# A selective scan on VectorE: two states in one scan over two PSUM banks, instead of one state over one bank

## The chip, the cores and the metric

One NeuronCore of a Trainium2 chip runs the whole program in one launch. The time is device microseconds of an execution, the median of three runs. The profile shows one further execution. Engines are named as the profile names them: PE is TensorE, DVE is VectorE, ACT is ScalarE, POOL is GpSimd, SP is SyncE, which issues the DMAs.

## The reference

Eight images of 96 channels and 64 x 64 pixels pass through a layer with a selective scan and then through attention and a feed-forward part. The scan takes nearly all the time. For each image there are four directions k (row order, column order, and both reversed), 192 channels d, 16 states n and 4096 positions:

```python
def step(hst, inp):
    u_i, dt_i, b_i, c_i = inp
    dA = jnp.exp(dt_i[..., None] * A)
    hst = dA * hst + (dt_i * u_i)[..., None] * b_i[:, :, None, :]
    y = jnp.einsum('bkdn,bkn->bkd', hst, c_i)
    return (hst, y)
h0 = jnp.zeros((bb, k, d, n), u.dtype)
_, ys = lax.scan(step, h0, (u_t, dt_t, b_t, c_t))
return ys.transpose(1, 2, 3, 0) + D[None, :, :, None] * u
```

Before it, per image, come a normalization, a projection, a depthwise convolution and the projections that give the step sizes dt, B and C ("front"). After it come a gate, two convolutions with a channel gate, attention, and a quantized feed-forward ("back end").

## The kernel before, in words

**Units, tiles, states, slots.** A *unit* is one direction of one image on one chunk of T = 512 positions: 8 images x 4 directions x 8 chunks = 256 units. A unit has six *tiles* n = 0 to 5 (`TILES`: g is a half of the states, j a third of the channels). The 128 partitions of a tile hold 64 channels twice, each half with other states, and its free axis holds G = 4 states m of 512 positions. So a unit has 24 *slots*, slot = 4n + m, and each slot is one scan of 128 x 512.

**The way of one state.**
- `inputs` (L952): POOL multiplies B by dt * u for all four states of a tile into an SBUF buffer `hb` (six buffers). It is issued two tiles ahead.
- `decays` (L1065): ACT writes exp(dt * A) of one state into one PSUM bank `da`, issued two slots ahead. There are three such banks.
- the scan (L1133): DVE runs h = da * h + hb along the 512 positions. A column of `carry` holds h from the chunk before. The first chunk of a direction starts from 0.
- the product with C: for some states DVE does it, right after the scan (L1135). Those are the *banked* states: their scan writes its result back into the PSUM bank `da`, and the product reads that bank and writes `hb`. For the other states the scan writes `hb`, and POOL later multiplies a tile's unbanked states in one instruction (`outputs`, L962).
- the carry: ACT copies the last column of each banked scan (L1136), or of a tile's unbanked scans together (L1141). These copies wait in `kept` and are issued at the beginning of the next slot.
- `sums` (L972): PE adds the states up with a matmul against `halves`, in PSUM banks y01 and y2. A last matmul adds D * u, or the sum of the directions before (`ident`), and `gather` (L993) has ACT copy the bank out for a DMA.

`BANKED` (L34) says how many states of each tile are banked: tiles 0, 2 and 4 all four, 1 and 3 none, tile 5 two, or one in the first eight units of images 1 to 7.

**Step sizes** (`step_sizes`, L911) have six steps i: a matmul into PSUM, then Abs, Exp and Ln on ACT (softplus), a combination on DVE, and dt * u on POOL. They come once a unit for 128 channels (kind "a") and once in two units for the other 64 of both (kind "b", in odd units). `spread` (L940) has SP copy the results within SBUF into the layout of the tiles. `states` loads B and C, `fetched_dt`, `fetched_u` and `fetched_pair` load what the step sizes need, `before` (L964) loads the operand of the last matmul.

**The order is written by hand.** `plan` (L1007) puts each of these calls for the unit `u`, its predecessor `last` and its successors `nxt` and `third` at a slot. The loop from L1102 issues, in each slot: the carry copies kept, the exp of two slots later, the scan, the product with C, and what the plan has there. Every engine takes its instructions in this order. After that `advance` lets two side streams go on: the front of the next image and the back end of the image before. They put a few matmuls, activations and DVE products into the slots. A side stream that needs another activation table waits for one of the slots `CALM = (0, 1, 8, 9, 16, 17)`, and then loads a table, runs Silu or Gelu, and loads the old table again. Before the units of the next image are fetched, the front of that image is drained.

[...] three for `da`, one for `dt` (step sizes), one each for f0 and f1 (side streams), y01 and y2.

Of the kernel before, what the change touches and what calls it, by code (L numbers as in the profile page):

```python
# [24 lines left out]
G = 4  # L25
# [8 lines left out]
BANKED = ((4, 0, 4, 0, 4, 1), (4, 0, 4, 0, 4, 2))  # L34
# [9 lines left out]
def kernel(ctx: ExitStack, tc: tile.TileContext, a, out):  # L44
# [16 lines left out]
    BANKS = {"da": 3, "dt": 1, "f0": 1, "f1": 1, "y01": 1, "y2": 1}  # L61
# [14 lines left out]
    one = const([P, 1], 1.0, "one")  # L76
    ones_c = const([C, C], 1.0 / C, "ones_c")
# [778 lines left out]
    for b in range(out.shape[0]):  # L856
        s = {"b": b, "done": set(), "live": b + 1 == out.shape[0]}
        images.append(s)
        for pair in (1, 0):
            for back in range(2):  # L860
                for i in range(NC):
                    u = Unit()
                    u.s, u.pair, u.back, u.k = s, pair, back, pair + 2 * back
                    u.c, u.start = (NC - 1 - i if back else i), i == 0
                    u.new, u.i = (pair, back, i) == (1, 0, 0), len(units)
                    u.bc, u.hb, u.delta, u.du = {}, {}, {}, {}
                    u.banked = BANKED[int(b == 0 or u.i % 32 >= NC)]
                    units.append(u)
# [42 lines left out]
    def step_sizes(us, i):  # L911

        u, which = us[0], "ab"[len(us) - 1]
        if i == 0:
            u.ps = bank("dt", "dt")
            if which == "a":
                todo = [(u.ps, slice(0, P), u)]
            else:
                todo = [(u.ps[64 * h : 64 * h + 64], slice(P, DI), w) for h, w in enumerate(us)]
            for ps, d, w in todo:  # L920
                nc.tensor.matmul(ps, dt_w[32 * w.k : 32 * w.k + R + 1, d], w.dts, start=True, stop=True)  # L921
            u.nat = sp.tile([P, T], F32, tag="nat" + which, name="nat", bufs=1)
            if which == "a":
                u.nata = u.nat
            else:
                for w in us:
                    w.natb = u.nat
        elif i == 1:
            nc.scalar.activation(u.nat, u.ps, AF.Abs)
        elif i == 2:  # L930
            nc.scalar.activation(u.nat, u.nat, AF.Exp, scale=-1.0)
        elif i == 3:
            nc.scalar.activation(u.nat, u.nat, AF.Ln, bias=one)  # L933
        elif i == 4:
            nc.vector.scalar_tensor_tensor(u.nat, u.ps, 0.0, u.nat, ALU.max, ALU.add)  # L935
        else:
            x = u.ua if which == "a" else u.ub
            nc.gpsimd.tensor_tensor(x, u.nat, x, ALU.mult)  # L938
# [19 lines left out]
    def outputs(u, n):  # L958

        lo = u.banked[n]  # L960
        hb = u.hb[n][:, lo:, :]
        nc.gpsimd.tensor_tensor(hb, hb, u.bc[1, TILES[n][0]][:, lo:, :], ALU.mult)  # L962

    def before(u):  # L964

        src = u.s["u"][1] if u.k == 1 else u.s["y"][u.pair]
        u.plain = []
        for i, rows in enumerate((slice(0, P), slice(P, src.shape[0]))):
            t = sp.tile([P, T], F32, tag=f"u{i}", name=f"u{i}", bufs=1)[: rows.stop - rows.start]
            u.plain.append(into(t, src[rows, bass.ts(u.c, T)]))  # L970

    def sums(u, ns, m):  # L972
# [12 lines left out]
        if ns[-1] == 5 and m == 1:  # L985
            first = u.k == 1
            for ps, w, x in (
                (u.p[0], dd_a if first else ident, u.plain[0]),
                (u.p[1][low] if first else u.p[1], dd_b if first else ident, u.plain[1]),
            ):  # L990
                nc.tensor.matmul(ps, w, x, start=False, stop=True, skip_group_check=True)  # L991
# [15 lines left out]
    def plan(u, last, nxt, third):  # L1007
# [6 lines left out]
        if last:  # L1014
            put(0, outputs, last, 5)
            put(0, before, last)
            for m in range(2):
                put(m, sums, last, (3, 4), 2 + m)
            for m in range(2):
                put(5 + m, sums, last, (5,), m)  # L1020
            put(7, states, u, 1, 1)
            put(10, gather, last, 0)
            put(11, gather, last, 1)
# [4 lines left out]
        if third and u.i % 2:  # L1028
            put(16, step_sizes, (nxt, third), 5)
        put(8, outputs, u, 1)  # L1030
        put(16, outputs, u, 3)
        for m in range(4):
            put(13 + m, sums, u, (0, 1), m)
            if m < 2:
                put(18 + m, sums, u, (2,), m)
                put(22 + m, sums, u, (3, 4), m)
        if nxt:
            for i, slot in enumerate((0, 2, 4)):
                put(slot, step_sizes, (nxt,), i + 3)
            put(4, spread, nxt, 0, (0, 1))  # L1040
            put(6, spread, nxt, 1, (0, 1))
# [6 lines left out]
        if third:  # L1048
            put(1, fetched_dt, third)
            put(9, fetched_u, third)  # L1050
            for i, slot in enumerate((20, 22, 23)):
                put(slot, step_sizes, (third,), i)
            if u.i % 2:
                for i, slot in enumerate((9, 11, 12, 13, 15)):
                    put(slot, step_sizes, (nxt, third), i)
                put(17, spread, nxt, 0, (2,))
                put(18, spread, nxt, 1, (2,))
            elif u.i + 3 < len(units):
                put(21, fetched_pair, third, units[u.i + 3])
        return at  # L1060

    def at_index(i):
        return units[i] if 0 <= i < len(units) else None

    def decays(q):  # L1065

        if q >= 24 * len(units):
# [3 lines left out]
        da[q] = bank("da", "da")  # L1071
        nc.scalar.activation(  # L1072
            da[q], u.delta[j], AF.Exp, scale=a_neg[:, u.k, j, g * G + m : g * G + m + 1]
        )

    da, kept, side, carry = {}, [], [], None
# [12 lines left out]
    for i in range(3):  # L1089
        step_sizes(units[1:2], i)  # L1090
# [3 lines left out]
    decays(1)  # L1094

# [6 lines left out]
    for u in units:  # L1102
# [13 lines left out]
        if third and third.new:  # L1116
            drained(*side[-1:])
            all_issued()
        if u.start:
            carry = sp.tile([P, 24], F32, tag="carry", name="carry")  # L1120
        todo = plan(u, last, nxt, third)
        for slot in range(24):
            n, m = divmod(slot, G)
            g, j = TILES[n]
            q, hb, first_at = 24 * u.i + slot, u.hb[n], 0 if u.back else T - 1
            col = carry[:, 8 * j + g * G + m : 8 * j + g * G + m + 1]
            while kept:
                kept.pop(0)()
            decays(q + 2)
            d = da.pop(q)  # L1130
            banked = m < u.banked[n]
            dd, x = (d[:, ::-1], hb[:, m, ::-1]) if u.back else (d, hb[:, m, :])
            nc.vector.tensor_tensor_scan(dd if banked else x, dd, x, 0.0 if u.start else col, ALU.mult, ALU.add)  # L1133
            if banked:
                nc.vector.tensor_tensor(hb[:, m, :], d, u.bc[1, g][:, m, :], ALU.mult)  # L1135
                kept.append(lambda col=col, d=d, at=first_at: nc.scalar.copy(col, d[:, at : at + 1]))  # L1136
            elif m == G - 1:
                lo = 8 * j + g * G
                kept.append(
                    lambda c=carry[:, lo + u.banked[n] : lo + G].unsqueeze(2), h=hb[:, u.banked[n] :, :], at=first_at:  # L1140
                    nc.scalar.copy(c, h[:, :, at : at + 1])  # L1141
                )
# [8 lines left out]
    before(u)  # L1151
    for m in range(2):
        sums(u, (3, 4), 2 + m)
    for m in range(2):
        sums(u, (5,), m)
    gather(u, 0)
# [79 lines left out]
```

## Time and profile before

| | us |
|---|---|
| median of three runs | 11327.45 (11326.49 to 11333.61) |
| profiled execution, its own time | 11335.55 |
| its span, first to last instruction | 11333.8 |
| first scan to last scan | about 352 to 11,091 |

| engine | busy us in the profile | what takes it |
|---|---|---|
| DVE | 10390.3 | 6144 scans, 3528 products with C |
| POOL | 10398.8 | 1536 input products, 768 output products |
| PE | 8544.5 | sums, side streams |
| ACT | 7478.7 | 6144 exps, carry copies, side streams |

A line of the groups reads: source line, engine, operation, tile written <- tiles read, shapes, count, then busy us and mean ns of one, then the engine's idle time just before such instructions and what ended most of it. A line of the waits reads: who waited <- for whom: us in total, times, longest. A line of the timeline: start, duration, engine, instruction. A line of the windows: stretch, its length, then the busy us of each engine with the number of its instructions, the granted TensorE clock, the share of the DMA engines and GB/s.

### The profile page before, as it was taken

How to read it: one execution, taken by the hardware profiler on the slowest of the kernel's cores; microseconds unless marked ns; L12 is line 12 of the kernel's file. 1: busy time of each engine (PE TensorE's matmuls, PEld its weight loads, DVE VectorE, ACT ScalarE, POOL GpSimd, SP SyncE). 2: the span in 40 equal slices, each digit the busy share in tenths (PEclk: the TensorE clock that was granted, in tenths of full speed). 3: DMA queues.
4: the chain of work that ended last, by engine and by line, in shares of the span. 5: the costliest groups of instructions: out<-in, count | busy, mean ns of one | idle time of the engine just before them, and what ended most of it. 6: DMA issues, size and time to landing. Idle time of an engine off the chain costs nothing. (4 is left out here: it accounts for less than half of the span.)

```text
span 11333.8 us, 97039 instructions
## 1 busy us (share of the span) xinstructions
PE 8544.5 (75%) x23270; PEld 2320.9 (20%) x23270; DVE 10390.3 (92%) x10868; ACT 7478.7 (66%) x14899; POOL 10398.8 (92%) x2783
## 2 busy tenths in 40 slices
PE   6577658887678876888678876788768877676677
PEld 2111112222122211222112221222212221111212
DVE  0799999999999999999999999999999999999993
ACT  3566656767666676667766676666766667666674
POOL 0799999999999999999999999999999999999991
PEclk8678878888788877889788887888878888787788
DMA  2788878898888888888888888889888888888883
GB/s 70 170 197 197 200 188 210 208 226 200 202 207 211 221 198 201 212 212 216 195 212 207 214 217 195 208 205 224 213 197 207 211 220 201 195 199 196 202 199 90
DMA packets 1081040, 2253.25 MB, mean 199 GB/s; under 512 B 419609, under 2 KB 420314, under 8 KB 949395
## 3 DMA queue, kind: packets, MB, share of 16 engines
q1 hardware_dynamic: 1080467, 2247.05, 81.5%
q8 instruction: 184, 3.01, 0.1%
q14 instruction: 389, 3.19, 0.1%
HBM read 1507.14 MB, written 336.69 MB: 163 GB/s over the span
## 5 line engine op out<-in xcount | busy, mean ns | idle before, releaser
L956 POOL TENSOR_TENSOR hb<-b,du 128x2048 f32<-128x2048 f32 x1536 | 6935.8, 4532 | 23.0 <-DMA du<-ua 16.0
L1072 ACT ACTIVATE da<-delta,w_a_logs 128x512 f32<-128x512 f32 x6144 | 4216.4, 689 | 696.7 <-DVE hb L1133 575.6
L982 PE MATMUL p<-hb,halves 128*64 128x512 f32 x12288 | 3813.9, 729 | 809.0 <-POOL hb L962 391.7
L1133 DVE TENSOR_TENSOR_SCAN da<-da,carry,hb 128x512 f32<-128x512 f32 x3087 | 3949.2, 1279 | 57.1 <-ACT da L1072 53.4
L962 POOL TENSOR_TENSOR hb<-hb,c 128x2048 f32<-128x2048 f32 (+2 forms) x768 | 2982.3, 3883 | 304.7 <-ACT carry L1141 262.6
L1133 DVE TENSOR_TENSOR_SCAN hb<-da,carry,hb 128x512 f32<-128x512 f32 x2289 | 2781.1, 1264 | 59.4 <-ACT da L1072 58.4
L1135 DVE TENSOR_TENSOR hb<-da,c 128x512 f32<-128x512 f32 x3528 | 2440.6, 692 | 153.9 <-DVE da L1133 0.9
L1136 ACT COPY carry<-da 128x1 f32<-128x1 f32 x3528 | 554.8, 157 | 2356.0 <-DVE hb L1135 2345.5
L982 PEld LDWEIGHTS p<-hb,halves 128*64 128x64 f32 x12288 | 914.5, 161 | 3556.5 <-issue 2126.2
L435 PE MATMUL conv<-f0im,taps 97*128 97x512 f32 (+1 forms) x2088 | 909.3, 669 | 89.8 <-ACT f0pre L491 50.3
L1133 DVE TENSOR_TENSOR_SCAN da<-da,hb 128x512 f32<-128x512 f32 x441 | 537.8, 1219 | 27.9 <-POOL hb L956 26.5
L938 POOL TENSOR_TENSOR ua<-nat,ua 128x512 f32<-128x512 f32 x256 | 326.7, 1276 | 257.6 <-DMA b<-xd 257.6
L935 DVE SCALAR_TENSOR_TENSOR nat<-dt,nat 128x512 f32<-128x512 f32 x384 | 259.5, 676 | 239.3 <-ACT nat L933 239.3
L921 PE MATMUL dt<-dts,dt_w 7*64 7x512 f32 (+1 forms) x1024 | 450.8, 660 | 18.8 <-DVE nat L935 14.3
L991 PE MATMUL p<-u,ident 128*128 128x512 f32 x768 | 436.0, 695 | 5.3 <-DMA u<-y 5.1
L376 PE MATMUL ctr<-f1b,cen_c 96*96 96x512 f32 x460 | 271.0, 695 | 198.8 <-DVE f1b L770 160.6
L435 PEld LDWEIGHTS conv<-f0im,taps 97*128 97x128 f32 (+1 forms) x2088 | 254.5, 175 | 676.4 <-issue 524.4
L1133 DVE TENSOR_TENSOR_SCAN hb<-da,hb 128x512 f32<-128x512 f32 x327 | 377.9, 1204 | 4.9 <-ACT da L1072 4.9
L382 PE MATMUL var<-f1b,ones_c 96*96 96x512 f32 x346 | 207.9, 685 | 152.6 <-ACT f1b L379 143.0
L1141 ACT COPY carry<-hb 128x4 f32<-128x4 f32 (+2 forms) x768 | 146.7, 191 | 197.3 <-DVE hb L1133 184.8
L656 PE MATMUL cab<-f1m,cab_w 96*96 96x512 f32 x348 | 206.0, 719 | 91.1 <-ACT f1b L665 41.7
L619 PE MATMUL cab<-f1im,cab_w 97*32 97x512 f32 x1044 | 264.7, 627 | 12.8 <-DMA f1im<-xld 7.9
(425 smaller groups left out, 7479.0 us busy)
## 6 DMA issues: line engine op xcount, KB each, us to landing
b<-xd SPq DMA_DIRECT2D x1024, 512.0 KB
c<-xd SPq DMA_DIRECT2D x1024, 512.0 KB
delta<-nat SPq DMA_DIRECT2D x1536, 128.0 KB
du<-ua SPq DMA_DIRECT2D x1024, 128.0 KB
y<-yt SPq DMA_DIRECT2D x512, 256.0 KB
u<-y SPq DMA_DIRECT2D x384, 256.0 KB
ua<-u SPq DMA_DIRECT2D x256, 256.0 KB
du<-ub SPq DMA_DIRECT2D x512, 128.0 KB
```

The lines of the kernel that those rows point to most:

```text
L376: nc.tensor.matmul(ps, cen_c, src, start=i == 0, stop=i == len(srcs) - 1)
L435: nc.tensor.matmul(ps, taps[:, t, lo : lo + n], im[:, r0 + dy : r0 + dy + 8, dx : dx + HW], start=t == 0, stop=t == 8,)
L921: nc.tensor.matmul(ps, dt_w[32 * w.k : 32 * w.k + R + 1, d], w.dts, start=True, stop=True)
L938: nc.gpsimd.tensor_tensor(x, u.nat, x, ALU.mult)
L956: nc.gpsimd.tensor_tensor(hb, u.bc[0, g], u.du[j].unsqueeze(1).to_broadcast([P, G, T]), ALU.mult)
L962: nc.gpsimd.tensor_tensor(hb, hb, u.bc[1, TILES[n][0]][:, lo:, :], ALU.mult)
L982: nc.tensor.matmul(ps, halves, u.hb[n][:, i, :], start=TILES[n][0] == 0 and m == 0, stop=False, skip_group_check=True)
L991: nc.tensor.matmul(ps, w, x, start=False, stop=True, skip_group_check=True)
L1072: nc.scalar.activation(da[q], u.delta[j], AF.Exp, scale=a_neg[:, u.k, j, g * G + m : g * G + m + 1])
L1133: nc.vector.tensor_tensor_scan(dd if banked else x, dd, x, 0.0 if u.start else col, ALU.mult, ALU.add)
L1135: nc.vector.tensor_tensor(hb[:, m, :], d, u.bc[1, g][:, m, :], ALU.mult)
L1136: kept.append(lambda col=col, d=d, at=first_at: nc.scalar.copy(col, d[:, at : at + 1]))
```

## The change

Banked states are taken in pairs. A tile `da` now holds two states over two PSUM banks, and two such tiles replace the three single banks. One scan of 1024 elements runs through both states, one product with C covers both, and one copy saves both carries; it is issued at the beginning of the slot after the pair's second one. So that the second state of a pair starts afresh, ACT adds its decay times its carry to its first input element and then sets that decay to 0. Unbanked states keep a scan each. Odd units (but for the first eight of images 1 to 7) have all four states of tile 5 banked, and no POOL product for it. The bank `dt` goes: step sizes use y01 and y2 between the gather of one unit and the sums of the next, and the plan is rearranged for that.

```diff
-BANKED = ((4, 0, 4, 0, 4, 1), (4, 0, 4, 0, 4, 2))
+BANKED = (((4, 0, 4, 0, 4, 2),), ((4, 0, 4, 0, 4, 2), (4, 0, 4, 0, 4, 4)))
...
-    BANKS = {"da": 3, "dt": 1, "f0": 1, "f1": 1, "y01": 1, "y2": 1}
+    BANKS = {"f0": 1, "f1": 1, "y01": 1, "y2": 1}
...
-                    u.banked = BANKED[int(b == 0 or u.i % 32 >= NC)]
+                    some = BANKED[int(b == 0 or u.i % 32 >= NC)]
+                    u.banked = some[u.i % len(some)]
...
-            u.ps = bank("dt", "dt")
+            u.ps = bank({"a": "y01", "b": "y2"}[which], "dt")
...
         lo = u.banked[n]
+        if lo == G:
+            return
```

The plan (moves of slot only; `added` is the last matmul of a bank, taken out of `sums`; `before` loads one bank's operand at a time):

```diff
         if last:
             put(0, outputs, last, 5)
-            put(0, before, last)
             for m in range(2):
                 put(m, sums, last, (3, 4), 2 + m)
+            put(2, added, last, 0)
+            put(4, gather, last, 0)
             for m in range(2):
                 put(5 + m, sums, last, (5,), m)
+            put(6, added, last, 1)
+            put(8, gather, last, 1)
             put(7, states, u, 1, 1)
-            put(10, gather, last, 0)
-            put(11, gather, last, 1)
+        if nxt:
+            put(2, spread, nxt, 0, (0, 1))
+            put(3, spread, nxt, 1, (0, 1))
+        if third:
+
+            put(5, fetched_u, third)
+            for i, slot in enumerate((6, 8, 9, 10, 12, 20)):
+                put(slot, step_sizes, (third,), i)
+            if u.i % 2:
+                for i, slot in enumerate((10, 12, 13, 14, 16, 17)):
+                    put(slot, step_sizes, (nxt, third), i)
...
-        for m in range(4):
-            put(13 + m, sums, u, (0, 1), m)
+        for m, slot in enumerate((15, 15, 16, 16)):
+            put(slot, sums, u, (0, 1), m)
             if m < 2:
-                put(18 + m, sums, u, (2,), m)
+                put(19 + m, sums, u, (2,), m)
                 put(22 + m, sums, u, (3, 4), m)
+        put(18, before, u, 0)
+        put(21, before, u, 1)
         if nxt:
-            for i, slot in enumerate((0, 2, 4)):
-                put(slot, step_sizes, (nxt,), i + 3)
-            put(4, spread, nxt, 0, (0, 1))
-            put(6, spread, nxt, 1, (0, 1))
...
-        if third:
-            put(1, fetched_dt, third)
-            put(9, fetched_u, third)
-            for i, slot in enumerate((20, 22, 23)):
-                put(slot, step_sizes, (third,), i)
-            if u.i % 2:
-                for i, slot in enumerate((9, 11, 12, 13, 15)):
-                    put(slot, step_sizes, (nxt, third), i)
                 put(17, spread, nxt, 0, (2,))
-                put(18, spread, nxt, 1, (2,))
...
+                put(19, spread, nxt, 1, (2,))
+        fourth = at_index(u.i + 3)
+        if fourth:
+            put(14, fetched_dt, fourth)
```

The front of the next image is drained when `units[u.i + 3]` is the first of an image, one unit earlier than before, and ahead of the loop all six step sizes of the second unit are taken, and `fetched_dt` of the third. The decays and the scan:

```diff
-        da[q] = bank("da", "da")
+        if m % 2 == 0:
+            da[q // 2] = psum.tile([P, 2, T], F32, tag="da", name="da", bufs=2)
+        d = da[q // 2]
         nc.scalar.activation(
-            da[q], u.delta[j], AF.Exp, scale=a_neg[:, u.k, j, g * G + m : g * G + m + 1]
+            d[:, m % 2, :], u.delta[j], AF.Exp, scale=a_neg[:, u.k, j, g * G + m : g * G + m + 1]
         )
+        if m % 2 and m < u.banked[n]:
+
+
+            i, at = (0, T - 1) if u.back else (1, 0)
+            edge, col = d[:, i, at : at + 1], column(j, g, m - 1 + i)
+            if not u.start:
+                x = u.hb[n][:, m - 1 + i, at : at + 1]
+                nc.scalar.activation(x, edge, AF.Identity, bias=x, scale=carry[0][:, col : col + 1])
+            nc.scalar.copy(edge, zero)
...
+    def scanned_state(u, slot):
...
+        banked = m < u.banked[n]
+        if banked and m % 2:
+            decays(q + 2)
+            return
+        while kept:
+            kept.pop(0)()
+        decays(q + 2)
+        pair = da[q // 2] if m % 2 == 0 else da.pop(q // 2)
+        if banked:
+            col = column(j, g, m + u.back)
+            d, x = (t.rearrange("p m l -> p (m l)") for t in (pair, hb[:, m : m + 2, :]))
...
+        nc.vector.tensor_tensor_scan(d if banked else x, d, x, init, ALU.mult, ALU.add)
+        if banked:
+            nc.vector.tensor_tensor(hb[:, m : m + 2, :], pair, u.bc[1, g][:, m : m + 2, :], ALU.mult)
```

## The prediction

> **What bounds the kernel now.** I read the busy table of the page first, then its groups.
>
> ```profile
> PE 8544.5 (75%) x23270; PEld 2320.9 (20%) x23270; DVE 10390.3 (92%) x10868; ACT 7478.7 (66%) x14899; POOL 10398.8 (92%) x2783
> ...
> L956 POOL TENSOR_TENSOR hb<-b,du 128x2048 f32<-128x2048 f32 x1536 | 6935.8, 4532 | 23.0 <-DMA du<-ua 16.0
> L1133 DVE TENSOR_TENSOR_SCAN da<-da,carry,hb 128x512 f32<-128x512 f32 x3087 | 3949.2, 1279 | 57.1 <-ACT da L1072 53.4
> ...
> L1135 DVE TENSOR_TENSOR hb<-da,c 128x512 f32<-128x512 f32 x3528 | 2440.6, 692 | 153.9 <-DVE da L1133 0.9
> L1136 ACT COPY carry<-da 128x1 f32<-128x1 f32 x3528 | 554.8, 157 | 2356.0 <-DVE hb L1135 2345.5
> ```
>
> DVE and POOL tie at 92%, and neither works before about 350 us or in the last 240 us: inside the scan stage both are nearly full. Which of the two leads is seen in the windows of 200 us (busy PE, PEld, DVE, ACT, POOL), one from image 0 and one from image 2:
>
> ```profile
> 900.00:1100.00 200.00, 137.63 (x380) 36.72 (x378) 193.81 (x199) 129.61 (x259) 199.02 (x53) 0.81 0.84 200
> 3100.00:3300.00 200.00, 158.85 (x397) 40.85 (x396) 187.39 (x194) 130.21 (x264) 186.88 (x48) 0.85 0.84 208
> ```
>
> In the first POOL has no room, in the second POOL waits too. The waits view says for whom:
>
> ```profile
> POOL hb L962 <- ACT carry L1141: 262.6, 206, 8.7
> ...
> PE p L982 <- ACT yt L1002: 311.4, 56, 13.0
> ```
>
> POOL's product waits for a carry copy, which waits for a scan: DVE leads, POOL follows closely. A unit is 24 scans: 40.2 us in image 0, 40.7 to 43.5 us in the others. VectorE's pace is read from its timeline, and the order behind it from ScalarE's (start, duration, instruction):
>
> ```profile
> 4999.55 1.28 DVE L1133 TENSOR_TENSOR_SCAN da<-da,carry,hb 128x512 f32<-128x512 f32 x1
> 5000.87 0.69 DVE L1135 TENSOR_TENSOR hb<-da,c 128x512 f32<-128x512 f32 x1
> 5001.48 1.28 DVE L1133 TENSOR_TENSOR_SCAN da<-da,carry,hb 128x512 f32<-128x512 f32 x1
> ...
> 5005.92 4.79 DVE L1133 TENSOR_TENSOR_SCAN hb<-da,carry,hb 128x512 f32<-128x512 f32 x4
> ```
>
> ```profile
> 5001.60 0.16 ACT L1136 COPY carry<-da 128x1 f32<-128x1 f32 x1 [1.04 <-DVE hb L1135]
> 5001.79 0.69 ACT L1072 ACTIVATE da<-delta,w_a_logs 128x512 f32<-128x512 f32 x1
> ```
>
> A banked state costs 1.93 us start to start (the product waits 0.04 us for its own scan; two independent instructions overlap by 0.08 us), an unbanked one (4.79 - 0.08)/4 = 1.178 us. ScalarE starts the copy 0.04 us after the product ends, the exp 0.19 us later.
>
> [...] the copy of the scan's last column waits for the *product*, 2345.5 us in all. [...] Here a tiny exp with one such operand (L690) takes 239 ns against 157 for the copy: 82 ns.
>
> **The change, part by part.**
>
> *Two states in one scan and one product.* Banked states: 3528 before. After: 56 units (the first eight of images 1 to 7) and the 100 other even units have 14, the 100 other odd ones 16: 784 + 1400 + 1600 = 3784, in 1892 pairs. The trace has no scan of 1024. At 512 a scan without carry operand takes 1204 ns [...]. So I take 1.067 us per 512 elements and 0.212 us fixed (0.06 of it the carry operand). Pair: scan 1.279 + 1.067 = 2.346; 0.04; [...] less 0.08: 3.535 us against 3.86. Bounds: 3.535, and 3.75 if the 0.212 goes with the elements.
> Before: 3528 x 1.93 + 2616 x 1.178 = 9891. After: 1892 x 3.535 + 2360 x 1.178 = 9468. **DVE -423 us**, on the path.
>
> *POOL* loses the tile-5 product in 100 units (2362 ns) and a state of it in 56 (3448 to 2362 ns): 236 + 61 = -297 us. In the scan stage (352 to 11,091 us) it then needs 10,372 - 297 = 10,075 us, and 595 us lie outside: a floor of 10,670 us. Per unit it needs 38.5 to 39.9 us, like VectorE (38.0 to 39.9 with its side work), so this cover is just enough; counted as nothing by itself.
>
> *New work on ScalarE.* Each pair gets an Identity of one column (1668; the 224 pairs of first chunks have none) and a copy of zero (1892, 0.16 us). The Identity has two pointer operands: 157 + 2 x 82 = 0.32 us (bounds 0.16 and 0.35). Carry copies fall from 3528 to 1892. Busy: 534 + 297 - 257 = +574 us, to about 8050 (71%). That is beside other work. What is not: **both exps and the edge must be done before a pair's scan starts**. Before, exp(q+2) gated scan q+2 alone, and a late exp(q+3) had a slot more.
> From the end of pair p-1's product: 0.04 + copy 0.19 + exp 0.69 + exp 0.61 + 0.03 + 0.32 + 0.03 + 0.16 + 0.04 = 2.11 us, with 3.535 - 0.08 = 3.455 us until VectorE wants pair p+1: 1.34 us of room. Behind two unbanked scans: 2 x 1.178 - 0.08 = 2.28, less 1.92 (no carry copy): 0.36 us. Into that room goes all that ScalarE is given in the *even* slot between the two exps. (In odd slots it comes after the edge.) I took ScalarE's rows between successive exps from the trace as side work per slot, added what the new plan puts there, gave back VectorE's own side work of the same two slots, and summed what exceeds the room: slot 0, 44 us; slot 6, 24; slot 8, 74 (gather and Abs now both there); slot 14, 55 (the Ln of odd units); slot 16, 73; the rest 12. **+282 us**, 151 of it in 56 even slots with a table switch: Silu 1.48 + 2 x 1.28 = 4.05 us, Gelu 0.68 + 2.57 = 3.25 us. Queued behind it on ScalarE: the second exp, the edge, the next carry copy; waiting for that: the scan, then POOL's product.
> The edge also waits for POOL's inputs of its tile. They end 3.5, 5.3 and 4.1 us (medians) ahead of the first scan of tiles 0, 2, 4, at the 5th percentile 1.3; the edge needs 0.6. Cost 0, at most +40.
>
> *Today's waits of the scans for exps:*
>
> ```profile
> DVE hb L1133 <- ACT da L1072: 63.3, 91, 1.5
> ...
> DVE da L1133 <- ACT da L1072: 53.4, 22, 6.3
> ```
>
> 117 us. Most lie in slots 11 to 15, where gathers, Abs, Exp and Ln crowd the unbanked tile; gathers leave it, the pair's step sizes stay: -40 (0 to -117).
>
> *PSUM.* The pairs take four banks for three, and "dt" moves into y01 and y2. Step sizes at slots 6 to 20 now sit between gather (4, 8) and sums (15, 19); their matmul waits for a gather two slots earlier, sums for a VectorE read three slots earlier: covered by those slots. Gathers move from 10 and 11 to 4 and 8. The first one's sums are long done there (their last matmul ends 7 us, median, before ScalarE gets to slot 4). The last matmul of slot 6 today ends 1.1 us before ScalarE gets to slot 8 in the median, but 0.7 us after it in the mean of the late ones over all units: ScalarE would stand there. PE itself wins: its wait for yt (311 us in the row above) goes, since sums start eleven slots after the gather. I take 0.3 us a unit, two thirds of it reaching VectorE: +50 (0 to +180), and -25 (0 to -100) for side matmuls that VectorE waits for.
>
> *SP and its DMAs.* Delta spreads leave at slot 2 with values finished at slot 12 of the unit before; du spreads at 3, behind POOL's product of slot 20. The wait of these spreads for nat, 1956 us on the queue, goes; VectorE's own product was far behind it, so 0 (to -30). The u load comes at 5 behind the spread that frees its single buffer; behind it nothing is needed before slot 10. The skip inputs load at slots 18 and 21 for use at 2 and 6: five or more slots, 8 us, for 256 KB. Their reads follow y writes issued at slots 7 and 11. Step-size rows come a unit earlier, hence the drain a unit earlier: the next image's front ends at unit 26.6 of 32, before 29: 0.
> *Head and tail.* Three ScalarE, one VectorE and one POOL instruction move ahead of the loop: under 4 us once.
>
> **Sum:** -423 + 282 - 40 + 50 - 25 = -156. The profiled execution took 11335.55 us (span 11333.8): 11,180. It lay 8 us above the median 11327.45, so 11,170.
>
> **Rivals.** *Full gain:* ScalarE's room suffices, since it has 30% idle time and VectorE's stalls refill it; for it, only 56 table switches are large; against it, an in-order engine can't use idle time later. -423 less up to 117: 10,787 to 10,911; POOL's floor of 10,670 allows it. *ScalarE's chain decides (slower):* place, the second exp and edge of each pair; price, twice my 0.15 us a pair (stalls shift the next copies, POOL's inputs come later as VectorE quickens, the gather stands for PE): -423 + 564 + 180 - 40 = +281, 11,610. It decides from 0.245 us a pair on, (423 + 40)/1892. For it: room of 0.36 us ahead of three pairs a unit. Against it: ScalarE has no side work in over two thirds of the slots. *The fixed cost is none:* a scan of 1024 takes 2.56 us: +401, 11,570[...].
>
> **Chances.** Forecast's band (10,980 to 11,300) 0.60; full gain 0.13; slower cases 0.18 (0.13 and 0.05); the rest about no change. A measurement here tells 0.2% (23 us) from nothing. Faster 0.71, same 0.08, slower 0.21. The range leaves out one in ten at each end: 10,920 to 11,400.
>
> **What would show it.** Pair scan rows near 2.35 us (the fixed cost), products near 1.225; DVE busy near 10,040, POOL 10,102, ACT 8050; waits of scans for the edge's zero copy of 250 to 400 us, long ones after Silu and Gelu; few waits of PE for yt. A pair scan over 2.45 us, or waits for the edge beyond 460 us, would make the forecast wrong on the slow side; under 100 us of them on the fast side.

## The result, and the profile after

The changed kernel takes 11359.19 us (median; 11357.41 to 11380.91) against 11329.91 us for the kernel before on the same chip: ratio 1.0029, 95% interval 1.0018 to 1.0040. It is **slower by 0.3%**, where the forecast was 1.4% faster. The profiled executions have spans of 11356.8 and 11333.8 us: +23.0 us, which the table below takes apart.

The busy table and the groups of the page of the changed kernel. Lines have moved: L1141 is the scan, L1143 the product with C, L1084 the exp, L1094 and L1095 the edge (the Identity and the zero), L1151 the carry copy.

```profile
PE 8547.8 (75%) x23270; PEld 2330.4 (21%) x23270; DVE 10088.4 (89%) x7341; ACT 8100.8 (71%) x16723; POOL 10106.6 (89%) x2683
...
L958 POOL TENSOR_TENSOR hb<-b,du 128x2048 f32<-128x2048 f32 x1536 | 6927.2, 4527 | 47.9 <-DMA du<-ua 19.2
...
L1141 DVE TENSOR_TENSOR_SCAN da<-da,carry,hb 128x1024 f32<-128x1024 f32 x1668 | 3918.7, 2349 | 463.3 <-ACT da L1095 264.1
...
L1141 DVE TENSOR_TENSOR_SCAN hb<-da,carry,hb 128x512 f32<-128x512 f32 x2040 | 2497.7, 1266 | 63.3 <-ACT da L1084 37.5
L1143 DVE TENSOR_TENSOR hb<-da,c 128x1024 f32<-128x1024 f32 x1892 | 2317.4, 1225 | 102.8 <-DVE da L1141 2.3
...
L1094 ACT ACTIVATE hb<-da,hb,carry 128x1 f32<-128x1 f32 x1668 | 586.4, 352 | 115.3 <-POOL hb L958 4.7
```

Read it beside the page of before. VectorE is busy 302 us less, POOL 292 us less, and the pair's two instructions have the length that was forecast (2349 ns for the scan, 1225 for its product). Both engines are at 89% now, where they were at 92%, and yet the time is nearly the same. What grew stands behind the last bar of the pair scan's line: VectorE is idle for 463.3 us before such scans. In the kernel before, the two scan lines with a carry had 57.1 us (shown in the prediction) and 59.4 us:

```profile
L1133 DVE TENSOR_TENSOR_SCAN hb<-da,carry,hb 128x512 f32<-128x512 f32 x2289 | 2781.1, 1264 | 59.4 <-ACT da L1072 58.4
```

The waits view of the changed kernel, VectorE alone (us in total, times, longest), says for whom the scans stand:

```profile
DVE da L1141 <- ACT da L1095: 271.1, 179, 5.5
...
DVE da L1141 <- issue: 140.1, 203, 2.9
...
DVE hb L1141 <- ACT da L1084: 39.3, 49, 3.2
DVE da L1141 <- POOL hb L958: 35.5, 22, 3.2
DVE da L1141 <- ACT carry L1151: 23.7, 25, 2.3
...
DVE hb L1141 <- ACT carry L1151: 22.2, 24, 3.7
```

Half is put down to the zero copy, the last thing ScalarE does for a pair. For 140 us the profile names nobody ("issue"); the rows of the trace place 64 us of them at the scan of slot 16, 51 us at that of slot 8 (both behind an unbanked tile) and 25 us at that of slot 0. The names are inferred, and the rows say more than they do: of the 477.8 us that VectorE is idle before pair scans, 470 us end 0.03 to 0.11 us after a zero copy, also where the view names nobody or POOL. Of the 22 waits put down to POOL (35.5 us), 21 end so. Nearly every late pair scan waited for its edge.

POOL's output product waits for scans through their carry copy: 157.3 us of waits name that copy (262.6 us before), and 419.1 us name nobody.

The sum, from the rows of both traces (idle times are those right before the instruction; "other" holds the head, the tail and VectorE's side work):

| us | before | after | difference |
|---|---|---|---|
| VectorE busy | 10390.3 | 10088.4 | -302 |
| idle before scans | 149.3 | 544.6 | +395 |
| idle before products with C | 153.9 | 102.8 | -51 |
| other idle | 640.3 | 621.0 | -19 |
| span | 11333.8 | 11356.8 | +23 |

Of the 544.6 us, 477.8 stand before pair scans and the rest before unbanked ones.

How such a wait comes about is seen in the timeline of the changed kernel (start, duration, instruction, idle time before it), ScalarE first and VectorE after it, around the pair scan of slot 10 in unit 195:

```profile
8572.79 0.69 ACT L1084 ACTIVATE da<-delta,w_a_logs 128x512 f32<-128x512 f32 x1
8573.85 0.58 ACT L1005 COPY yt<-p 128x512 f32<-128x512 f32 x1 [0.37 <-PE p L978]
8575.85 0.60 ACT L931 ACTIVATE nat<-dt 128x512 f32<-128x512 f32 x1 [1.42 <-PE dt L923]
8576.34 0.58 ACT L379 ACTIVATE f0e<-ctr 96x512 f32<-96x512 f32 x1
8576.82 0.58 ACT L380 COPY f0e<-ctr 96x512 f32<-96x512 f32 x1
8577.28 0.70 ACT L1084 ACTIVATE da<-delta,w_a_logs 128x512 f32<-128x512 f32 x1
8578.02 0.35 ACT L1094 ACTIVATE hb<-da,hb,carry 128x1 f32<-128x1 f32 x1
8578.40 0.16 ACT L1095 COPY da<-zero 128x1 f32<-128x1 f32 x1
```

```profile
8575.01 1.23 DVE L1143 TENSOR_TENSOR hb<-da,c 128x1024 f32<-128x1024 f32 x1
8578.60 2.36 DVE L1141 TENSOR_TENSOR_SCAN da<-da,carry,hb 128x1024 f32<-128x1024 f32 x1 [2.37 <-ACT da L1095]
```

The first exp of the pair is done at 8573.5. Then ScalarE copies out a bank (standing 0.37 us for PE), takes the Abs of the step sizes (standing 1.42 us for their matmul) and two activations of a side stream, and only then the second exp and the edge. VectorE, free at 8576.23, stands 2.37 us. One part of those 3.8 us is ScalarE's work, another its own standing for PE ahead of the second exp.

### The profile page after: what moved, and what is told of

Read it like the earlier page. It is cut to its first block, busy times and chain, and to the rows that moved or that the text cites. A ratio compares the mean times of both kernels' runs of the same rounds, so it can differ in the third digit from the quotient of the medians.

```text
span 11356.8 us, 96229 instructions
## 1 busy us (share of the span) xinstructions
PE 8547.8 (75%) x23270; PEld 2330.4 (21%) x23270; DVE 10088.4 (89%) x7341; ACT 8100.8 (71%) x16723; POOL 10106.6 (89%) x2683
## 5 line engine op out<-in xcount | busy, mean ns | idle before, releaser
L1084 ACT ACTIVATE da<-delta,w_a_logs 128x512 f32<-128x512 f32 x6144 | 4227.5, 689 | 411.5 <-DVE hb L1141 282.3
L1141 DVE TENSOR_TENSOR_SCAN da<-da,carry,hb 128x1024 f32<-128x1024 f32 x1668 | 3918.7, 2349 | 463.3 <-ACT da L1095 264.1
L966 POOL TENSOR_TENSOR hb<-hb,c 128x2048 f32<-128x2048 f32 (+1 forms) x668 | 2685.6, 4020 | 646.6 <-issue 419.1
L1141 DVE TENSOR_TENSOR_SCAN hb<-da,carry,hb 128x512 f32<-128x512 f32 x2040 | 2497.7, 1266 | 63.3 <-ACT da L1084 37.5
L1143 DVE TENSOR_TENSOR hb<-da,c 128x1024 f32<-128x1024 f32 x1892 | 2317.4, 1225 | 102.8 <-DVE da L1141 2.3
L1151 ACT COPY carry<-da 128x2 f32<-128x2 f32 x1892 | 298.1, 158 | 1774.9 <-DVE hb L1143 1770.2
L923 PE MATMUL dt<-dts,dt_w 7*128 7x512 f32 (+1 forms) x1024 | 504.0, 737 | 262.8 <-ACT yt L1005 135.6
L1094 ACT ACTIVATE hb<-da,hb,carry 128x1 f32<-128x1 f32 x1668 | 586.4, 352 | 115.3 <-POOL hb L958 4.7
L1141 DVE TENSOR_TENSOR_SCAN da<-da,hb 128x1024 f32<-128x1024 f32 x224 | 512.0, 2286 | 14.5 <-ACT da L1095 7.0
L937 DVE SCALAR_TENSOR_TENSOR nat<-dt,nat 128x512 f32<-128x512 f32 x384 | 257.6, 671 | 261.6 <-ACT nat L935 240.4
L1141 DVE TENSOR_TENSOR_SCAN hb<-da,hb 128x512 f32<-128x512 f32 x320 | 373.3, 1206 | 3.5 <-ACT carry L1151 1.7
L1095 ACT COPY da<-zero 128x1 f32<-128x1 f32 x1892 | 308.0, 163 | 59.6
L1005 ACT COPY yt<-p 128x512 f32<-128x512 f32 x384 | 222.2, 579 | 79.9 <-PE p L978 79.5
```

The lines of the kernel that those rows point to most:

```text
L1084: nc.scalar.activation(d[:, m % 2, :], u.delta[j], AF.Exp, scale=a_neg[:, u.k, j, g * G + m : g * G + m + 1])
L1094: nc.scalar.activation(x, edge, AF.Identity, bias=x, scale=carry[0][:, col : col + 1])
L1095: nc.scalar.copy(edge, zero)
L1141: nc.vector.tensor_tensor_scan(d if banked else x, d, x, init, ALU.mult, ALU.add)
L1143: nc.vector.tensor_tensor(hb[:, m : m + 2, :], pair, u.bc[1, g][:, m : m + 2, :], ALU.mult)
```

## The experiments

Four theories were on the table after the result, and a fifth came later.
- **EVEN**: what the even slots give ScalarE between the two exps of a pair delays the second exp and the edge.
- **EDGE**: the edge instructions themselves, and their wait for POOL's inputs, cost the time.
- **PLAN**: the rearranged plan (gathers, step sizes in y01 and y2) costs it, whatever the pairs do.
- **UNIT**: odd units with all of tile 5 banked overload VectorE, and the even ones can't give it back. Mean unit times of the trace speak for it: 41.43 and 42.49 us (even, odd) before, 40.94 and 43.18 after.
- **PORT** comes with its run.

All ratios are to the kernel before on the same chip, with their 95% interval; differences to the changed kernel are taken through these ratios.

### The pairs' two exps together

```diff
         if banked and m % 2:
-            decays(q + 2)
             return
...
-        decays(q + 2)
+        if m % 2 == 0:
+            decays(q + 2)
+            decays(q + 3)
```

> Both exps of the next pair and its edge are issued at the beginning of the even slot, ahead of what the plan and the side streams give ScalarE in that slot; nothing else changes. Theory EVEN (scans of pairs wait because ScalarE's other work of the even slot stands between the two exps): the waits of pair scans fall from 464 us to about 200, the time from 11,359 to about 11,100 us. Theory UNIT (odd units with 16 banked states overload VectorE and POOL) and theory PLAN (gathers at slots 4 and 8 make ScalarE stand for TensorE): 11,330 to 11,360, no change, since neither the load nor the gathers move.

11178.74 us, **0.9868** (0.9851 to 0.9884): 1.6% faster than the change as made, with the same instructions. Waits view of this kernel, VectorE alone (L1142 is the scan):

```profile
DVE hb L1142 <- ACT da L1084: 85.5, 59, 5.3
...
DVE da L1142 <- issue: 56.4, 67, 2.7
DVE da L1142 <- ACT carry L1152: 53.0, 51, 4.4
DVE da L1142 <- ACT da L1095: 43.8, 35, 2.2
```

The wait for the zero copy falls from 271.1 to 43.8 us, all idle time before pair scans from 477.8 to 179.4. That is EVEN. How much of it is ScalarE's work in between, and how much its standing for PE, this run does not separate. The time stays some 80 us above the 11,100 expected, for it is not all gain: unbanked scans now wait 85.5 us for their exp (39.3 in the changed kernel), which comes behind what was put off; and the "other" idle time of VectorE grows from 621 to 729 us.

### The plan alone

The new plan, with the step sizes in y01 and y2, but with one state to a scan, no edge, three `da` banks, and the banked states of the kernel before (a part of the edit is shown):

```diff
-BANKED = (((4, 0, 4, 0, 4, 2),), ((4, 0, 4, 0, 4, 2), (4, 0, 4, 0, 4, 4)))
+BANKED = (((4, 0, 4, 0, 4, 1),), ((4, 0, 4, 0, 4, 2),))
...
-        if m % 2 == 0:
-            da[q // 2] = psum.tile([P, 2, T], F32, tag="da", name="da", bufs=2)
-        d = da[q // 2]
+        da[q] = psum.tile([P, T], F32, tag="da", name="da", bufs=3)
...
-        if banked and m % 2:
-            decays(q + 2)
-            return
```

> The new plan, with dt in y01 and y2, but one state to a scan, three da banks and the banked states of the kernel before. Theory PLAN: slower than before by what the pairs hide, 11,450 or more, with ScalarE standing for TensorE at the gathers. Theory EVEN: about the time before, 11,280 to 11,340, since every exp has its own slot again. Theory UNIT: the same, for the states of the units are those of before.

11262.63 us, 0.9939 (0.9924 to 0.9954). PLAN falls: the plan by itself *gains* 0.6%, 70 us. The waits view of this kernel, scans alone:

```profile
DVE da L1122 <- ACT da L1082: 46.8, 36, 3.6
DVE hb L1122 <- ACT da L1082: 24.5, 35, 3.3
```

The same two rows had 53.4 and 63.3 us before. ScalarE stands for PE here too (65.4 us before the gather's copy), and the scans wait less than before all the same: exp(q+2) is issued ahead of it and exp(q+3) has a slot more. So the new plan gains where a scan needs a single exp, and the loss comes with the pairs as the change orders them. The lower granted clock is no rival: it was 0.826 before, 0.816 after and 0.819 here, where the time falls. Measured from here, pairs and the 256 added banked states lose about 100 us.

### Fourteen banked states in all these units

```diff
-BANKED = (((4, 0, 4, 0, 4, 2),), ((4, 0, 4, 0, 4, 2), (4, 0, 4, 0, 4, 4)))
+BANKED = (((4, 0, 4, 0, 4, 2),), ((4, 0, 4, 0, 4, 2),))
```

> The changed kernel with 14 banked states in every unit, so that POOL multiplies two states of tile 5 in all units. VectorE has 118 us less to do, POOL 236 us more. Theory UNIT: faster, about 11,200, and odd and even units differ only by the step sizes of kind b. Theory EVEN: the waits in slots 2, 10 and 18 stay, POOL rises to 40.2 us a unit, the time is 11,330 to 11,420.

11341.4 us, 1.0007 (0.9998 to 1.0016): 0.2% below the changed kernel, where UNIT expected about 11,200. UNIT falls as the main cause. The same edit on top of the exps together:

> Both exps and the edge first, with 14 banked states in every unit. It prices the 256 further states with the waits for ScalarE mostly gone. If POOL is then the near bound, as its 40.2 us a unit says: slower by 60 to 100 us than with 16, about 11,260. If the states are worth nothing (as in the changed kernel, where 14 and 16 differ by 18 us): 11,170 to 11,190.

11246.67 us, 0.9928 (0.9913 to 0.9943), 68 us slower than with sixteen. Where ScalarE's order costs less, POOL's relief is worth something: in this kernel the Identity stands 115.4 us for POOL's inputs, in the changed kernel 4.7 us. The added states pay only once the stall is smaller.

### No edge

The lines from `if m % 2 and m < u.banked[n]:` to `nc.scalar.copy(edge, zero)` are taken out, so the second state of a pair goes on from the end of the first.

> The changed kernel without the Identity and the copy of zero, so the second state of each pair goes on from the first one's end instead of its own carry: this part of the computation is left out. Theory EDGE (the two small instructions and their wait for POOL are what is lost): the waits of pair scans fall below 150 us, the time to about 11,050. Theory EVEN: the room grows by about 0.5 us a pair, the waits fall by some 40%, 11,150 to 11,250. Theory PLAN: under 60 us gained.

11121.82 us, 0.9816 (0.9801 to 0.983), some 240 us less than the changed kernel. The time lies between what EDGE (11,050) and EVEN (11,150 to 11,250) had expected. Waits before pair scans fall from 477.8 to 295.0 us, not below 150, so EDGE is not the whole cause; but it is a large part, for leaving the edge out is worth more than the order of the exps (180 us). The two are parts of one chain: the edge is its last 0.6 us, and it is late because of what stands ahead of it. Without the edge every pair has that much more room, and most of what remains waits for the exps (L1132 is the scan):

```profile
DVE da L1132 <- ACT da L1084: 206.4, 136, 5.0
```

### The work in odd slots

Two ways of moving work away from between the exps, with the exps left where the change has them. The second gather and the step sizes move to odd slots where the plan allows it:

```diff
-            put(8, gather, last, 1)
+            put(9, gather, last, 1)
...
-            for i, slot in enumerate((6, 8, 9, 10, 12, 20)):
+            for i, slot in enumerate((6, 9, 9, 11, 12, 20)):
...
-                for i, slot in enumerate((10, 12, 13, 14, 16, 17)):
+                for i, slot in enumerate((10, 13, 13, 15, 16, 17)):
```

> The changed kernel with the plan's ScalarE work of slots 8 to 14 in odd slots: second gather at 9; Abs, Exp, Ln of kind a at 9, 9, 11; of kind b at 13, 13, 15. Theory EVEN: the wait of the pair of slot 10 falls from 148 us to about 50, that of slot 16 by some 30, the time to about 11,240. Theory PLAN (ScalarE stands for TensorE at the second gather and at Abs): the stand stays about 100 us, one slot later, and the time gains under 50 us.

11248.75 us, 0.9928 (0.9914 to 0.9943), 1.0% faster than the changed kernel. The waits before the scan of slot 10 fall from 149 to 48 us, at slot 16 from 92 to 59. A handful of slot numbers is worth over 110 us.

And the table switches of the side streams, in odd slots only (with 0.6 for 1 a waiting stream asks in every slot, so that it misses none of the three):

```diff
-    CALM = (0, 1, 8, 9, 16, 17)
+    CALM = (1, 9, 17)
...
         while place[0] is not None and place[0] not in CALM:
-            yield 1
+            yield 0.6
```

> The changed kernel with CALM = (1, 9, 17), odd slots alone, and a waiting side stream that looks in every slot; so Silu and Gelu with their table loads come behind the edge of the next pair. Theory EVEN: in the changed kernel 178 us of scan waits follow such a block, the most of it at slots 2, 10 and 18 (140 us); those fall below 30 us, and the time to about 11,230. Theory PLAN: the same time as the changed kernel within 30 us, since no gather or matmul moves.

11400.96 us, 1.0064 (1.0049 to 1.0079): a miss, slower than the change. The waits before the scans of slots 2, 10 and 18 did fall, from 256 to 128 us, as EVEN said. But those at 4, 12 and 20 rose from 59 to 169 us, and VectorE was 83 us busier. The groups of the kernel before and of this one, shapes kept apart, say with what:

```profile
L694 DVE TENSOR_SCALAR dgate<-ident,gate 96x96 f32<-96x96 f32 x8 | 17.6, 2206 | 0.3
```

```profile
L695 DVE TENSOR_SCALAR dgate<-ident,gate 96x96 f32<-96x96 f32 x8 | 109.1, 13632 | 0.3
```

This instruction of the back end comes once an image. The timelines of this kernel, VectorE and then POOL, show one of its eight:

```profile
2313.48 15.62 DVE L695 TENSOR_SCALAR dgate<-ident,gate 96x96 f32<-96x96 f32 x1
2329.03 2.28 DVE L1141 TENSOR_TENSOR_SCAN da<-da,hb 128x1024 f32<-128x1024 f32 x1
```

```profile
2305.47 8.99 POOL L958 TENSOR_TENSOR hb<-b,du 128x2048 f32<-128x2048 f32 x2
2314.41 4.51 POOL L966 TENSOR_TENSOR hb<-hb,c 128x2048 f32<-128x2048 f32 x1
2318.88 4.49 POOL L958 TENSOR_TENSOR hb<-b,du 128x2048 f32<-128x2048 f32 x1
2323.33 1.26 POOL L940 TENSOR_TENSOR ua<-nat,ua 128x512 f32<-128x512 f32 x1
2324.55 4.49 POOL L958 TENSOR_TENSOR hb<-b,du 128x2048 f32<-128x2048 f32 x1
```

It lasts from inside one product of POOL through four more instructions (five in all; the expectation below says three), and ends at 2329.10, 0.07 us after POOL's run of them ends (2329.04). The other six long ones, of 15.4 to 15.6 us, end in the same way. **PORT**: VectorE's product stands behind POOL's instructions until their run ends, here for 15.62 us. By what means they hold it up no run shows. If PORT is right, the same kernel with this product on ScalarE has EVEN's gain:

```diff
-            nc.vector.tensor_scalar(dgate, ident[:C, :C], gate, None, ALU.mult)
+            nc.scalar.activation(dgate, ident[:C, :C], AF.Identity, scale=gate)
```

> The kernel with table blocks in odd slots (11,401 us), and the small 96x96 product dgate moved from VectorE to ScalarE. In that kernel this one VectorE instruction took 15.4 to 15.6 us seven times, 109 us in all, through three POOL instructions in a row; in the changed kernel it took 2.4. Theory PORT (VectorE stood behind POOL there, and that hid what the odd slots gain): about 11,300, so 92 us less than with it on VectorE, and about 60 less than the changed kernel. Theory EVEN wrong on table blocks: 11,380 to 11,400, no change, the time lies elsewhere.

11283.37 us, 0.9965 (0.9951 to 0.9979): 1.0% faster than without this edit, 0.6% faster than the changed kernel. Groups of this kernel:

```profile
L695 ACT ACTIVATE dgate<-ident,gate 96x96 f32<-96x96 f32 x8 | 3.0, 375 | 5.2 <-DVE gate L694 5.2
```

Odd table switches gain, and PORT had hidden it. The product itself took 17.1 us in the changed kernel, so moving it can account for a part of the gain over that kernel, not for all. The gain is also smaller than EVEN had promised for odd switches (11,230): of the 81 us by which this span is shorter than that of the changed kernel, waits before scans are 30 us.

### Going on from the exps together

Four versions were meant to take away what was left of the waits there. None of them beat it.

*Later step sizes* (steps "a" at slots 6, 10, 11, 12, 14, 20, "b" at 11, 13, 14, 15, 17, 18, the second gather at 9):

> The version with both exps and the edge first, and the plan one or two slots later: second gather at 9, Abs, Exp, Ln, combination of kind a at 10, 11, 12, 14, kind b at 11 to 18. If what was left there comes from ScalarE standing for TensorE at gather and Abs (33 us and the 77 us of scan waits at slot 12): about 11,110. If it is ScalarE's load alone: 11,160 to 11,180, no change.

11311.35 us, 0.9985 (0.9977 to 0.9992): a miss by 200 us. The waits view of this kernel:

```profile
DVE hb L1142 <- ACT da L1084: 225.5, 155, 4.1
```

With the exps together alone it was 85.5. The scan of slot 14, in the unbanked tile 3, waits 160 us where it waited 6 there: with scans of 1.18 us ahead of it there is little room, and ScalarE's step sizes now lie in front of its exp. The same with table switches in slots 0, 1, 18 and 19:

> The same with CALM = (0, 1, 18, 19), slots in which the plan gives ScalarE nothing. In the version with both exps first 102 us of scan waits follow a table block, at slots 12 and 20: those fall by two thirds, another 60 us, to about 11,050, unless the front of the next image then ends so late that its drain stops the scans.

11415.9 us, 1.0074 (1.0058 to 1.0091): a miss; the same row has 228.1 us, 99 us of waits stand at slot 22, and PORT is back (84.8 us of `dgate`).

*Steps "b" in slots 12, 16, 17, 18, 19, 20*, with the sums and the spread that follow them two to four slots later:

> Both exps and the edge first, and the step sizes of kind b moved out of the unbanked tile 3 into tile 4: matmul at 12, Abs, Exp, Ln at 16, 17, 18, combination at 19, POOL's product at 20; sums of tile 2 at 21 and 22. Behind unbanked scans the room on ScalarE is 0.36 us, behind banked pairs 1.34 us. If that difference decides: the 77 us of waits at slot 12 and the 47 at slot 16 fall by half, the time to about 11,110. If only the order of exps and other work matters: 11,170 to 11,190.

11208.87 us, 0.9896 (0.9882 to 0.9911): 30 us slower than the exps together, though the waits of scans fell from 276 to 211 us. The groups of VectorE with the exps together, and of this kernel, give the other side:

```profile
L937 DVE SCALAR_TENSOR_TENSOR nat<-dt,nat 128x512 f32<-128x512 f32 x384 | 257.1, 670 | 257.6 <-ACT nat L935 237.9 <-DMA du<-ub 19.6
```

```profile
L937 DVE SCALAR_TENSOR_TENSOR nat<-dt,nat 128x512 f32<-128x512 f32 x384 | 257.9, 672 | 356.3 <-ACT nat L935 265.9 <-ACT carry L1152 69.8 <-DMA du<-ub 20.0
```

VectorE's own step of the step sizes follows ScalarE's Ln by one slot, and now stands 99 us more for it. The wait has moved from the scans to the instruction between them. With table switches in slots 0, 1, 8 and 9 alone, and the gate product on ScalarE:

> The same with table blocks at slots 0, 1, 8, 9 alone, where two pairs follow before an exp is needed that waits behind the block, and with dgate on ScalarE: 38 events at slots 16 and 17 cost 50 us at slot 20 in the version with both exps first; about 40 us of it goes, 11,070.

11239.79 us, 0.9923 (0.9908 to 0.9938): a miss. Waits of scans rise again, from 211 to 306 us, while L937's fall back; which of the moved switches makes them was not taken apart.

## Why the prediction was wrong, step by step

**What held.** *The instructions.* The scan has a fixed cost that two states share: the pair's scan takes 2349 and 2286 ns with and without a carry operand, 2.346 us forecast; the product 1225 ns, as forecast. The forecast's split of the scan, 1.067 us for 512 elements and 0.212 fixed, was the author's estimate: no scan of before has another length. The two kernels together show 2349 - 1279 = 1070 ns for 512 more elements, which leaves 209 of the 1279. For the product the trace of before has two lengths: 692 ns at 512 and 1959 at 1728 elements (L227, on 97 partitions), and the line through them gives 1225 at 1024; 533 ns for 512 leave 159. The Identity takes 352 ns against 0.32 us, forecast from 82 ns for an operand by pointer, which was the author's estimate from L690 and the copy; with its two such operands it takes 352 - 158 = 194 ns more than the carry copy of a pair, 97 for each if all of it is theirs. The zero copy takes 163 ns; ScalarE's busy time came to 8100.8 us (about 8050 forecast), POOL's to 10106.6 (10,102). The rival "the fixed cost is none", which had a scan of 1024 at 2.56 us, is out: 2.349 us were measured. Beforehand only the author's estimate of the fixed part stood against it. *The mechanism.* The forecast said that both exps and the edge must be done before a pair's scan, and that what ScalarE gets in the even slot between the exps uses up the room. Runs with the same instructions in another order take up to 180 us less, so it is this order that costs. *The rival's place and threshold.* "ScalarE's chain decides" was to turn the sign from 0.245 us of waits a pair on. The trace has 477.8/1892 = 0.253 us: just past it, and the result is just past zero. That the two lie so close is in part luck: the threshold sets 423 + 40 = 463 us of gains against the waits, and the runs have 302 + 51 + 19 + 82 = 454 us, made up of other parts (82 us are waits of before that went away). The rival's price, 0.30 us and more with the other scans and the standing for PE, was too high. *POOL's inputs.* The edge's wait for them was put at 0, at most 40 us; the Identity waited 4.7 us for them.

**The term that failed is the sum of the waits.** It put +282 for the even slots, +50 for the gather standing for PE and -40 for the waits of before: +292 net. Measured: +395. Before pair scans 332 us were counted and 478 measured; of the 149 us of waits before, 82 went away (67 are left, before unbanked scans), where 40 were counted. By slot of the side work, against the waits of the pair scan two slots later:

| side work in slot | forecast us | waits at the pair of slot | measured us |
|---|---|---|---|
| 0 | 44 | 2 | 36 |
| 6 | 24 | 8 | 55 |
| 8 | 74, and 50 for the gather | 10 | 149 |
| 14 | 55 | 16 | 92 |
| 16 | 73 | 18 | 71 |
| rest | 12 | 0 and 20 | 74 |
| (unbanked scans) | 77, left of today's 117 | 4, 6, 12, 14 | 67 |

The measured column adds up to the 544 us of the sum above. Slots 0 and 16, where table switches weigh most, were right to 8 us. What is short lies in three places. *The room behind unbanked scans.* It was known to be 0.36 us, at slots 8 and 16, and still underpriced: 147 us against 24 + 55 = 79. *The pairs at 0 and 20.* Each slot's excess was counted against the pair two slots later alone, and these pairs were taken as almost free; 74 us stand there, where 12 were counted for them and all the other slots. A backlog that lasts past the next pair would do this; no run isolates it. *Standing for PE at a second place.* The forecast let the gathers wait for their matmul, 0.3 us a unit or 77 us, and 79.5 us were measured. But the Abs behind them waits too, for the matmuls of the step sizes: 35.3 us in all, which the sum did not have. In the timeline above this is the longer of the two. PE takes those matmuls right behind the one that the gather waited for, and there they last 2.07 us (8573.74 to 8575.81).

**The gain was mis-sized too.** VectorE's work and its product gaps fell by 302 + 51 = 353 us, not 423. The forecast gave every start its overlap of 0.08 us with the instruction before. A start that waits has none: 679 scans start late, 209 before, and 470 x 0.08 = 38 us. So each such wait costs 0.08 us more than the idle time that it shows. Most of the rest can be located. The forecast took all banked scans of before at 1.28 us, but the 441 of first chunks took 1.219 (27 us); and it let a product wait 0.04 us for its scan, where the pairs' products wait 102.8/1892 = 0.054 us (27 us) and those of before 153.9/3528 = 0.044 (13 us the other way). Two slips of the sums are small: 2.346 + 0.04 + 1.225 - 0.08 is 3.531 us and not 3.535, 8 us over all pairs; and the range of the rival "full gain" counts one end from the median and the other from the span, which lie 6 us apart.

**The plan was worth 70 us, not 15,** as long as exps had a slot each: that is the run of the plan alone. In the forecast its terms nearly cancelled: +50 for the gather against -40 and -25.

**What the named indicators did.** "Waits for the zero copy of 250 to 400 us" came true by the view's name (271.1), and would have confirmed the forecast; by the rows 470 us of waits end at a zero copy, past the 460 that was to show it wrong. A forecast on waits is better put by the instruction that waits than by the releaser, since 140 us here have no releaser's name. Few waits of PE for the gather's copy at the sums came true; they went to the matmul of the step sizes (135.6 us of PE), for which ScalarE's Abs then stands.

**What stays open.** The best version that does the whole computation still has 275.6 us of waits before scans; its successors did not make it faster, and one of them only moved the waits to another instruction. How much of the stall is ScalarE's work and how much its standing for PE was not separated. Why table switches moved to slots 8 and 9 bring waits back was not settled.

## What to carry to other kernels

Fusing two instructions pays a fixed cost once instead of twice (here 209 ns for a scan, 159 for a product), but the fused one starts when the *later* of its inputs is ready (470 of the 477.8 us before pair scans end within 0.11 us of a zero copy's end). A producer that takes its instructions in the order of issue, as ScalarE does when it stands 1.42 us for a matmul with the second exp three instructions behind, makes that input late: issue all that one consumer instruction needs together, ahead of anything else, and only then count the gain (here the same instructions are 0.3% slower or 1.3% faster by that alone). Work out the room behind the *shortest* consumers in front of it, and count against it not only the producer's work but each place where it stands for a third engine. When a stretch moves and the time does not fall, add up the idle time before *every* instruction of the engine that leads, not before the one that was in the way.

## What the runs showed of the hardware

A product of 96x96 (`tensor_scalar`, SBUF to SBUF) takes 0.3 us on VectorE in the last image, where POOL is idle, and 2.4 or 2.5 us in seven images of the kernels before and after, each time until 0.07 us after the end of the POOL instruction that was under way. With the table switches in odd slots it took 15.4 to 15.6 us in those seven, through five instructions of POOL in a row: it did not end between POOL's instructions, only 0.07 us after the last of them. That is not shown to be a rule. In the kernel with later step sizes and switches in slots 0, 1, 18 and 19, four of the seven took 15.3 to 18.6 us, again through five, but three took 5.1 us, and in one of these three POOL's next instruction followed without a gap in the trace. On ScalarE the same product takes 375 ns.
